# A gate ahead of a query product, and a mixture's step behind a projection, in an attention and mixture-of-experts block

## The chip, the cores and the metric

The kernel runs on one core of a Trainium2 chip. The metric is device microseconds of one execution, as the median of several runs. Before the change three runs gave 1143.45 us as their median (1142.99 to 1148.04). Engines are named as in the profile: PE is TensorE (PEld its weight loads), DVE is VectorE, ACT is ScalarE, POOL is GpSimd, SP is SyncE, whose queue issues most DMAs.

## The reference

The input x has 8 sequences of 512 tokens and 512 channels, in float32. All of the work below is done in float32, but for the lists of the sort.

```
xn = layernorm(x)
q, k, v = rotate(silu(xn @ Wq)), rotate(silu(xn @ Wk)), xn @ Wv     # 16 heads of 32
o  = decayed linear attention in chunks of 128 tokens:
     scores = (q @ k.T) * D ; state S = lam * S + (k * decay).T @ v
     o = scores @ v + (q * decay) @ S
gate = xn @ Wg1 @ Wg2
s  = rmsnorm_per_head(o * sigmoid(gate)) * weight @ Wo
f  = sum over the 4 best of 16 experts of weight * swiglu(xn) + shared expert * sigmoid(..)
out = x + s * silu(f)
```

## The kernel before, in words

The kernel has four stages. First, all tokens are normed, routed and sent through the shared expert, beside sequence 0's attention. Second, sequence 1's attention runs, and beside it `table` builds the lists that sort tokens into blocks of one expert: VectorE compares (L526, L529, L533), ScalarE numbers (L542), PE multiplies (L565, a bank "a" or "d" for each of eight rounds) and VectorE adds the result up (L576 for the first round, L574 later). Third, the experts' blocks run. Fourth, sequences 2 to 7 run their attention, and beside it GpSimd gathers the experts' results for each tile of 128 tokens.

The attention of a sequence b goes through four groups g of four heads. `key` and `query` (both through `rotated`) make a product of four steps on PE (pk, pq, L659), a Silu on ScalarE (L669) and four VectorE instructions (L671 to L675). `by_token` transposes keys (L691) into the one kept bank "k", which also holds the states' products (L714); the states' scan is L729. `scores` fills four banks "a" (ps, L725), which VectorE empties with the decay mask (sc, L750). `output` makes po (L761 or L766, then L772) in a bank "d", and VectorE multiplies it with the gate in L776. `value` makes pv (L615). `gate_2` makes the four tiles of the gate (L645, named p in the profile) in four banks and ScalarE puts a Sigmoid of each into `on` (L649).

PSUM has eight banks under four tags: four "a", one "k", one "m" (key products, first expert products, even value tiles), two "d" (query products, outputs, projections, odd value tiles, rounds 3 and 5 of the lists). A new tile takes a free bank of its tag or waits until the old tile's readers are done.

The order on PE is written out by hand: everything under `on_pe()` is chained behind what was emitted before it. On the other engines, what is emitted under `behind(engine)` follows the last instruction emitted for that engine; the rest is placed by a list scheduler. Between the steps of a product in sequence 1, `between[0]()` advances `table` by one piece.

In stage four the attention of a sequence calls `step` (here `advance`) at places of its own. Each call moves every active tile's `mixture` on by one piece: four gathers (L1325), one in each of four calls, a GpSimd add (L1331), a second add (L1334) with a VectorE combination (L1336), a VectorE add (L1340), a Silu (L1343), and for the tiles of sequences 0 and 1 the end `last`, with VectorE's L1363. New tiles are started at five in eleven calls. The projection of sequence b-1 is put off into sequence b: `project_tiles(before, ...)` makes pw (L817) of one tile in a bank "d" and `finish` calls `last`, whose L1363 multiplies the mixture's result by pw and so frees the bank. The output's add (L1367, GpSimd) is put on a list `late` with the number of steps so far, and is issued by the second call of `advance` after that.

For each group the order in `sequence` is: `scores`, a step, the next key (or value), `by_token`, one deferred projection (groups 0 and 1), a step, the next query (or value), [the gate, in group 0, where it has not been made], a second deferred projection, `output`, a step. Only sequences 0 and 1 make the gate here; sequence 2's is made at the beginning of the blocks, and from sequence 3 on the gate is made at the end of the sequence before.

Of the kernel before, what the change touches and what calls it, by code (L numbers as in the profile page):

```python
# [38 lines left out]
FIRST = 2  # L39
# [58 lines left out]
def tile_block(ctx: ExitStack, tc: tile.TileContext, a: dict, out: bass.AP):  # L98
# [8 lines left out]
    def bank(tag, name):  # L107
        return pp.tile([P, 512], F32, tag=tag, name=name, bufs={"a": 4, "k": 1, "m": 1, "d": 2}[tag])
# [101 lines left out]
    @contextmanager  # L210
    def on_pe():

        with tc.issue_after(last_pe[-1]) if last_pe else nullcontext():
            yield
        traced = nc.cur_bb.bb.instructions
        last_pe.append(next(
            i for i in reversed(traced) if i.engine == mybir.EngineType.PE))
# [374 lines left out]
    def home(b):  # L592
        return other[0] if other and (b - FIRST) % 2 else att

    def load_xT(b, pool=None):
        xT = (pool or home(b)).tile([P, KC, N], F32, tag="xT", name=f"xT_{b}", bufs=1)
        nc.sync.dma_start(xT.rearrange("p k n -> p (k n)"), xT_d[b])
        xT_of[b] = xT
# [4 lines left out]
    v_of, on_of, kT_of, qT_of, qd_of, sc_of, st_of, g1_of, rs_of, kd_of = ({} for _ in range(10))  # L603
# [5 lines left out]
    def value(b, t):  # L609
        if t == 0:  # L610
            v_of[b] = att.tile([P, NC, D], F32, tag="v", name=f"v_{b}", bufs=2)
        pv = bank("d" if t % 2 else "m", f"pv_{b}_{t}")
        for k in range(KC):
            with on_pe():
                nc.tensor.matmul(  # L615
                    pv, lhsT=xT_of[b][:, k, t * P : (t + 1) * P], rhs=wv[:, k, :],
                    start=(k == 0), stop=(k == KC - 1))
            between[0]()
        nc.scalar.copy(v_of[b][:, t, :], pv)
# [16 lines left out]
    def gate_2(b, tiles=range(NC), banks="aaaa"):  # L636
        if 0 in tiles:
            on_of[b] = home(b).tile([P, G, N], F32, tag="on", name=f"on_{b}", bufs=1)
        g1 = g1_of[b]
        p2s = {t: bank(banks[t], f"p2_{b}_{t}") for t in tiles}  # L640
        with on_pe():
            for g in range(G):
                for t in tiles:
                    tq = slice(t * Q, (t + 1) * Q)
                    nc.tensor.matmul(  # L645
                        p2s[t][:, g * P : (g + 1) * P], lhsT=wg2[tq, g * P : (g + 1) * P],
                        rhs=g1[tq, :], start=True, stop=True)
        for t in tiles:
            nc.scalar.activation(  # L649
                on_of[b][:, :, t * P : (t + 1) * P],  # L650
                p2s[t].rearrange("p (g n) -> p g n", n=P), AF.Sigmoid)
        if NC - 1 in tiles:
            g1_of.pop(b)
# [24 lines left out]
    def key(b, g, ps=None):  # L678
        kT_of[g] = rotated(b, g, "k", wk, ps)

    def query(b, g):
        qT_of[g] = rotated(b, g, "q", wq)

    def by_token(b, g):

        if not kept:
            kept.append(bank("k", f"pk_{b}_{g}"))
        pk = kept[0]
        with on_pe():
            for c in range(NC - 1):  # L690
                nc.tensor.transpose(  # L691
                    pk[:, c * P : (c + 1) * P], kT_of[g][:, c * C : (c + 1) * C], ident)
        kd = scr[0].tile([P, NC - 1, HG, HD], F32, tag="kd", name=f"kd_{b}_{g}")
        by_chunk = pk[:, : (NC - 1) * P].rearrange("p (c h d) -> p c h d", c=NC - 1, d=HD)
        for j in range(HG):
            nc.scalar.activation(
                kd[:, :, j, :], by_chunk[:, :, j, :], AF.Copy,
                scale=dk[:, g * HG + j : g * HG + j + 1])
        kd_of[g] = pk[:, (NC - 1) * P :], kd
# [55 lines left out]
    def output(b, g):  # L755
        po = bank("d", f"po_{b}_{g}")
        st, qd, sc = st_of.pop(g), qd_of.pop(g), sc_of.pop(g)
        with on_pe():
            for c in range(1, NC):
                if carry:  # L760
                    nc.tensor.matmul(  # L761
                        po[:, c * C : (c + 1) * C], lhsT=st[:, c - 1, :], rhs=qd[:, c - 1, :],
                        start=(c == 1), stop=False)
                for j in range(0 if carry else HG):
                    hs = slice(j * HD, (j + 1) * HD)
                    nc.tensor.matmul(  # L766
                        po[hs, c * C : (c + 1) * C], lhsT=st[hs, c - 1, :], rhs=qd[hs, c - 1, :],
                        start=(c == 1), stop=False)
            for c in range(NC):
                for j in range(HG):  # L770
                    h = g * HG + j
                    nc.tensor.matmul(  # L772
                        po[j * HD : (j + 1) * HD, c * C : (c + 1) * C],
                        lhsT=v_of[b][:, c, h * HD : (h + 1) * HD],
                        rhs=sc[j][:, c], start=False, stop=(c == NC - 1))
        nc.vector.tensor_tensor(on_of[b][:, g, :], po, on_of[b][:, g, :], ALU.mult)  # L776
# [16 lines left out]
    def inverse(b):  # L793
        nc.vector.reciprocal(rs_of[b], rs_of[b])
# [18 lines left out]
    def project(b, t):  # L813
        pw = bank("d", f"pw_{b}_{t}")
        with on_pe():
            for g in range(G):
                nc.tensor.matmul(  # L817
                    pw, lhsT=on_of[b][:, g, t * P : (t + 1) * P], rhs=wo[:, g, :],
                    start=(g == 0), stop=(g == G - 1))
        return pw  # L820
# [36 lines left out]
    def sequence(b, step, projected, before=None, defer=False, also=lambda: None):  # L857


        n = b + 1  # L860

        def project_tiles(q, ts):
            if q is not None:
                for t in ts:
                    projected(q, t, project(q, t))


        fill = ([0], [1], [2], [3], [], [], [], [])
        for g in range(G):
            scores(b, g)  # L870
            late_step = b == 0 and g + 2 >= G
            if not late_step:
                step()
            if g + 2 < G:
                key(b, g + 2)
            else:
                value(n, 2 * (g - 2))
            if late_step:
                step()
            if g + 1 < G:  # L880
                by_token(b, g + 1)
            project_tiles(before, fill[2 * g])
            step()
            if g + 2 < G:
                query(b, g + 2)
                if g + 3 == G and n not in xT_of:
                    load_xT(n)
            if g + 2 == G:
                value(n, 1)
            if g == 0 and b not in on_of:  # L890
                gate_2(b)
            project_tiles(before, fill[2 * g + 1])
            if fill[2 * g + 1] == [NC - 1]:
                on_of.pop(before, None)
            output(b, g)
            if defer and g + 2 == G:
                gate_1(n)
            step()
        v_of.pop(b)
        if n == FIRST:  # L900
            for _ in range(4):
                next(filling)
            gate_1(n)
            next(filling, None)
            for e in range(E - LATE // 2, E):
                nc.sync.dma_start(wexp[:, e, :], a["experts"][:, e, :])
            squares(b)
            inverse(b)
            value(n, 3)
            normed(b)  # L910
            experts_of_blocks()
            return
        if defer:
            gate_2(n)
        value(n, 3)
        also()
        squares(b)
        step()
        inverse(b)
        key(n, 0)  # L920
        also()
        query(n, 0)
        normed(b)
        also()
        if not defer:
            step()
        key(n, 1)
        by_token(n, 0)
        if defer:
            step()  # L930
        query(n, 1)
        also()
        if not defer:
            gate_1(n)
            project_tiles(b, [0, 1])
            also()
            project_tiles(b, [2, 3])
            also()
            on_of.pop(b)
        step()  # L940
# [156 lines left out]
    along()  # L1097
    enter(0, along)
    sequence(0, along, spill, also=lambda: next(sorting, None))
    for _ in sorting:  # L1100
        pass
# [14 lines left out]
    next(filling)  # L1116
    between[0] = lambda: next(filling, None)
    sequence(1, lambda: None, spill)
    between[0] = lambda: None
    slot = slots[0]  # L1120
# [354 lines left out]
```

## Time and profile before

| | |
|---|---|
| median of three runs | 1143.45 us (1142.99 to 1148.04) |
| the profiled execution | 1133.33 us |
| its span | 1131.5 us |
| PE busy | 1109.5 us (98%) |
| DVE busy | 753.3 us (67%) |
| ACT busy | 427.6 us (38%) |
| POOL busy | 446.2 us (39%) |
| sequence 1's first group to its last list product, about | 224 to 279 us |
| stage four's sequences 2 to 7, about | 689 to 1130 us |

A line of a timeline gives start and duration in us, engine, line, operation, output<-input and shape; in square brackets stands the idle time of the engine before it and who ended that. A line of the waits gives engine, its tile and line, whom it waited for, the total in us, how often, and the longest. A line of a window gives its bounds, its length, then for each of PE, PEld, DVE, ACT and POOL the busy time and in brackets the count; then the granted TensorE clock as a share of full speed, the share of the DMA engines, and GB/s. The timeline joins neighbouring instructions of one kind; a matmul's end is modelled, so times from one start to the next start are the safer measure.

### The profile page before, as it was taken

To read this page: it belongs to the slowest core of one execution; us is meant where nothing else is said; L and a number is where in the kernel's file an instruction comes from. 1 tells how busy PE (TensorE), PEld (TensorE's weight loads), DVE (VectorE), ACT (ScalarE), POOL (GpSimd) and SP (SyncE) were. 2 spreads that over 40 slices of the span, in tenths; PEclk is the share of its full clock that TensorE was granted. 3 is DMA by queue.
4 is the path that set the end of the run, shared out by engine and by line. 5 is a ranking of instruction groups with operands and counts; after the bars stand their busy time and mean duration, and the time that the engine had idled before them with its cause. 6 is when DMAs were issued, how large, how long until landed. Compare 5 with 4: busy or idle time off the path is not lost. (4 is left out here: it accounts for less than half of the span.)

```text
span 1131.5 us, 21658 instructions
## 1 busy us (share of the span) xinstructions
PE 1109.5 (98%) x7838; PEld 682.4 (60%) x7838; DVE 753.3 (67%) x1608; ACT 427.6 (38%) x924; POOL 446.2 (39%) x430
## 2 busy tenths in 40 slices
PE   7999999999999999999999999999999999999998
PEld 4445554455577777777777885655645545546453
DVE  6357744998354455555555666978789597797774
ACT  3223525255433333333333442352432523423541
POOL 4312100200333333333332314836868858768111
PEclk9999999999999999999999999999999999999999
DMA  9895341192779999999999986714648537444012
GB/s 343 311 334 187 138 161 48 57 378 88 215 208 237 236 234 238 234 239 239 241 238 267 245 203 244 270 57 160 232 121 258 156 114 250 138 138 143 11 38 75
DMA packets 163932, 218.50 MB, mean 193 GB/s; under 512 B 89840, under 2 KB 99184, under 8 KB 161776
## 3 DMA queue, kind: packets, MB, share of 16 engines
q1 hardware_dynamic: 142704, 146.76, 42.0%
q0 software_dynamic: 21120, 70.34, 24.2%
q8 instruction: 64, 1.05, 0.4%
q14 instruction: 44, 0.36, 0.1%
HBM read 126.78 MB, written 72.43 MB: 176 GB/s over the span
## 5 line engine op out<-in xcount | busy, mean ns | idle before, releaser
L1226 PE MATMUL pgu<-xts,wst 128*128 128x256 f32 x896 | 202.6, 379 | 0.0
L1226 PEld LDWEIGHTS pgu<-xts,wst 128*128 128x128 f32 x896 | 170.1, 190 | 46.2 <-issue 13.4
L1325 POOL DMA_INDIRECT yg<-y_d,place x128 | 141.6, 1106 | 30.3 <-issue 19.1
L1157 POOL DMA_INDIRECT more<-xn_d,slot x69 | 65.5, 949 | 220.1 <-DVE w L1210 107.5
L1241 PE MATMUL py<-wexp,slb 128*128 x272 | 129.9, 593 | 0.0
L1245 DVE TENSOR_SCALAR y<-py,w 128x512 f32<-128x512 f32 x136 | 102.0, 751 | 41.8 <-PE py L1241 35.4
L615 PE MATMUL pv<-wv,xT 128*128 128x512 f32 x256 | 118.3, 603 | 0.0
L659 PE MATMUL pk<-xT,wk 128*128 128x512 f32 x256 | 118.1, 603 | 0.0
L659 PE MATMUL pq<-xT,wq 128*128 128x512 f32 x256 | 115.7, 593 | 0.5 <-PEq L1289 0.5
L1232 ACT ACTIVATE slb<-pgu 128x256 f32<-128x256 f32 (+1 forms) x80 | 28.1, 351 | 219.8 <-PE pgu L1226 216.4
L817 PE MATMUL pw<-wo,on 128*128 128x512 f32 x224 | 102.3, 604 | 5.1 <-DVE m L1363 4.3
L1157 POOL DMA_INDIRECT xg<-xn_d,slot x67 | 63.6, 949 | 98.8 <-DVE w L1210 44.0
L1233 DVE TENSOR_TENSOR slb<-slb,pgu 128x256 f32<-128x256 f32 (+1 forms) x80 | 30.5, 381 | 105.3 <-ACT slb L1232 101.4
L1367 POOL TENSOR_TENSOR xo<-xo,m 128x512 f32<-128x512 f32 x31 | 45.6, 1470 | 134.2 <-DVE m L1363 126.7
L1208 DVE COPY wst<-wexp 128x512 f32 x160 | 61.7, 426 | 41.0 <-DVE y L1245 24.5
L1190 ACT COPY xts<-pl 128x512 uint16<-128x512 uint16 x110 | 84.3, 769 | 0.3 <-DMA pl<-xg 0.2
L659 PEld LDWEIGHTS pq<-xT,wq 128*128 128x128 f32 x256 | 47.2, 190 | 54.4 <-issue 53.0
L750 DVE TENSOR_TENSOR sc<-ps,dmask 128x512 f32<-128x512 f32 x128 | 79.0, 676 | 0.9 <-PE ps L725 0.9
L659 PEld LDWEIGHTS pk<-xT,wk 128*128 128x128 f32 x256 | 46.2, 189 | 50.7 <-issue 48.3
L615 PEld LDWEIGHTS pv<-wv,xT 128*128 128x128 f32 x256 | 45.9, 190 | 49.7 <-issue 46.7
L817 PEld LDWEIGHTS pw<-wo,on 128*128 128x128 f32 x224 | 41.8, 193 | 55.5 <-issue 46.2
L734 ACT COPY blocked<-state 32x96 f32<-32x96 f32 x96 | 30.8, 321 | 83.0 <-DVE state L729 82.2
(193 smaller groups left out, 1728.4 us busy)
## 6 DMA issues: line engine op xcount, KB each, us to landing
y_d<-y SPq DMA_DIRECT2D x136, 256.0 KB
wexp<-in_experts SPq DMA_DIRECT2D x16, 768.0 KB
sh_d<-sh SPq DMA_DIRECT2D x32, 256.0 KB
xT<-xT_d SPq DMA_DIRECT2D x8, 1024.0 KB
m<-sh_d SPq DMA_DIRECT2D x32, 256.0 KB
xo<-in_x SPq DMA_DIRECT2D x32, 256.0 KB
out<-xo SPq DMA_DIRECT2D x31, 256.0 KB
x<-in_x SPq DMA_DIRECT2D x7, 1024.0 KB
```

The lines of the kernel that those rows point to most:

```text
L615: nc.tensor.matmul(pv, lhsT=xT_of[b][:, k, t * P : (t + 1) * P], rhs=wv[:, k, :], start=(k == 0), stop=(k == KC - 1))
L659: nc.tensor.matmul(ps, lhsT=w[:, k, g * P : (g + 1) * P], rhs=xT_of[b][:, k, :], start=(k == 0), stop=(k == KC - 1))
L750: masked[:] = [nc.vector.tensor_tensor(s, pss[j].rearrange("p (c t) -> p c t", t=C), dmask[:, g * HG + j].unsqueeze(1).to_broadcast([P, NC ...
L817: nc.tensor.matmul(pw, lhsT=on_of[b][:, g, t * P : (t + 1) * P], rhs=wo[:, g, :], start=(g == 0), stop=(g == G - 1))
L1157: nc.gpsimd.indirect_dma_start(out=row(i), out_offset=None, in_=xn_d, in_offset=bass.IndirectOffsetOnAxis(ap=slot[:, i : i + 1], axis=0))
L1190: (nc.vector.tensor_copy if j in by_dve else nc.scalar.copy)(xt[:, u, KP:, :].bitcast(U16).rearrange("p k (t h) -> p h k t", h=2), pls[j % ...
L1208: nc.vector.tensor_copy(to, wflat[:, bass.ds(off + u * KC * F, KC * F)])
L1226: nc.tensor.matmul(pg[:, o * n * P : (o + 1) * n * P], lhsT=wst[j % 2][k // KP][:, (k % KP * 2 + o) * F :][:, :F], rhs=xt[:, :, k, :], sta ...
L1241: nc.tensor.matmul(py, lhsT=hT[:, u * P : (u + 1) * P], rhs=wflat[:, bass.ds(off + KC * 2 * F, D)], start=True, stop=True)
L1245: gone.append(nc.vector.tensor_scalar(y, py, w[:, u : u + 1], None, ALU.mult).ins)
L1325: nc.gpsimd.indirect_dma_start(out=yg, out_offset=None, in_=y_d, in_offset=bass.IndirectOffsetOnAxis(ap=place[:, r, g : g + 1], axis=0))
L1367: nc.gpsimd.tensor_tensor(xo, xo, m, ALU.add)
```

## The change

Two places of `sequence` are edited.

In sequences 3 to 6 (`b > FIRST`, FIRST is 2), in group 0, the step that stood right behind `scores` is taken from there and made behind the first deferred projection and its `last`, directly ahead of the step that already stood there. The number of steps is the same, and so are the tiles' pieces in each step, but for the output's add of the first projection, which goes by the number of steps and so is issued one step earlier.

In sequence 1, the gate is made ahead of query (1,2) and not behind it, and its fourth tile takes the bank "m" of the key products in place of a fourth bank "a". The old call is still there and finds the gate made. In sequence 0, where `b` is zero, nothing is changed.

```diff
         for g in range(G):
             scores(b, g)
             late_step = b == 0 and g + 2 >= G
-            if not late_step:
+            behind_tile = b > FIRST and g == 0
+            if not late_step and not behind_tile:
                 step()
             if g + 2 < G:
                 key(b, g + 2)
...
             if g + 1 < G:
                 by_token(b, g + 1)
             project_tiles(before, fill[2 * g])
+            if behind_tile:
+                step()
             step()
+            if g == 0 and b and b not in on_of:
+                gate_2(b, banks="aaam")
             if g + 2 < G:
                 query(b, g + 2)
```

## The prediction

> **What bounds the kernel now.** I read the page's busy times and chain first, then TensorE's waits, then timelines and clock windows around the two places that the diff touches.
>
> ```profile
> PE 1109.5 (98%) x7838; PEld 682.4 (60%) x7838; DVE 753.3 (67%) x1608; ACT 427.6 (38%) x924; POOL 446.2 (39%) x430
> PE 27%; DVE 10%; issue 1%; ACT 1%; DVEq 0%
> PE pw L817 <- DVE m L1363: 4.3, 4, 1.9
> PE p L645 <- DVE wexp L576: 1.4, 1, 1.4
> ```
>
> PE is busy for nearly the whole span, so a reorder can win only what PE loses in waits, and what the clock loses behind them. TensorE's waits list two that concern the diff: the second sequence's gate (p, L645), once 1.4 us, and the deferred projection (pw, L817), four times, 4.3 us together.
>
> Place one, sequence 1, from PE's timeline, a clock window and VectorE's timeline:
>
> ```profile
> 234.26 0.71 PE L645 MATMUL p<-g,wg 32*128 32x128 f32 x8
> 236.33 1.15 PE L645 MATMUL p<-g,wg 32*128 32x128 f32 x24 [1.37 <-DVE wexp L576]
> 237.42 0.92 PE L766 MATMUL po<-qd,state 32*32 32x128 f32 x24
> 239.00:240.00 1.00, 1.00 (x28) 0.92 (x24) 1.00 (x3) 1.00 (x3) 0.00 (x0) 0.50 0.99 412
> 245.56 0.42 DVE L526 TENSOR_TENSOR wexp<-count,sp 128x512 f16<-128x512 f16 x1 [0.54 <-PE pn L565]
> 277.87 1.13 PE L565 MATMUL pn<-wexp 128*64 128x286 f16 x8 [0.80 <-DVE wexp L529]
> ```
>
> A quarter of the gate runs, then waits until L576 has copied the list product pn out of the bank that the gate's fourth tile needs. Start to start it takes 237.42-234.26 = 3.16 us; the gate of sequence 6 takes 1.10 (965.13 to 966.23). So 2.06 are lost, and then the granted clock is 0.5 (sixth number): the next po, state and score products take 4.61 us start to start (237.42 to 242.03), the same three later 3.09 (265.33 to 268.42), 1.52 more. But VectorE is busy for 24.00 and 24.96 us of the windows 225:250 and 250:275, and PE meets it again at 277.87.
>
> Place two, sequences 4 and 6: PE, then VectorE.
>
> ```profile
> 848.10 3.70 PE L817 MATMUL pw<-wo,on 128*128 128x512 f32 x8 [1.14 <-DVE m L1363]
> 865.75 3.70 PE L817 MATMUL pw<-wo,on 128*128 128x512 f32 x8 [0.15 <-DVE m L1363]
> 1001.48 5.40 PE L817 MATMUL pw<-wo,on 128*128 128x512 f32 x8 [1.91 <-DVE m L1363]
> 865.01 0.68 DVE L1363 TENSOR_TENSOR m<-m,pw 128x512 f32<-128x512 f32 x1
> 997.53 0.74 DVE L1336 SCALAR_TENSOR_TENSOR m<-m,sg,yg 128x512 f32<-128x512 f32 x1
> 1000.74 0.68 DVE L1363 TENSOR_TENSOR m<-m,pw 128x512 f32<-128x512 f32 x1
> ```
>
> The second projection waits for VectorE's L1363 to free the first one's bank. A pq or pw takes 3.44 us to the next start, so the true waits are 1.30 (sequence 4: 843.36+3.44 to 848.10), 1.29 (sequence 5: 919.20 to 923.93) and 2.07 (sequence 6: 995.97 to 1001.48); sequence 3 has none. Only the 2.07 is followed by half clock: that pw takes 5.23 to the next start against 3.53 in sequence 4, 1.70 more.
>
> **The change part by part.** No instruction is added or dropped; I take the order of each engine's queue from the code.
>
> *The gate.* It now follows the transposes that end at 229.4. Its three banks are score banks, freed by L750 one by one until 229.2; the fourth is the keys' bank, free when ScalarE's Silu (229.30, 0.60) ends at 229.9. Behind the gate on PE are queued query (1,2), its pn and po, so at most 0.5 us is new wait. The pn product then takes the fourth score bank and nobody waits for L576. PE gains up to 2.06+1.52 = 3.58. VectorE does not: from 221.6 to 277.8 it waits twice, 0.33 at 236.94 (for the Silu of that query) and 0.54 at 245.56 (for pn). The second goes, since pn comes earlier. The first stays, since the query now ends at 234.3+1.8 = 236.1, about where its Silu ran (236.30). So PE reaches 277.87 early and waits longer there. I take 0.54 gained. The best bound is 0.87 with both idles gone, or 3.58 if VectorE's order were not what ends it. The worst: the gate's Sigmoid now sits between two Silus, so a table load (row at 236.91, 1.28) may fall between pq and its Silu, which would cost VectorE 1.28-0.54 = 0.74, and the longer wait at 277 may bring half clock (1.52): 2.26 lost.
>
> The page "ScalarE: Activation LUTs", What ACT_TABLE_LOAD costs, speaks against this order: it puts a switch of tables at about 2.66 us, load and drain. The trace has the Sigmoid at 238.21, right behind the load; by the page the loss would be 1.38 larger, by the trace it is not.
>
> *The step.* In sequences 3 to 6 one step moves from before key (b,2) to behind the first projection's L1363. Its VectorE rows, start to start: sequence 3 L1340 (767.29) 0.61; sequence 4 L1363 and L1336 (843.09 to 844.36) 1.27; sequence 5 L1336 (918.94 to 920.66) 1.72; sequence 6 L1336 (997.53 to 998.20) 0.67. By that much L1363 comes earlier. Sequence 5's wait of 1.29 goes, sequence 4's 1.30 nearly, sequence 6's becomes 2.07-0.67 = 1.40.
>
> Where does it go? In sequence 4 VectorE's rows touch from 826.87 to 865.69, and the instructions before the third projection's L1363 (865.01) are the same in both orders; PE waits there until 865.75 either way. I take 0. Sequence 5 is the same: the state scan L729 (934.19), behind which the transposes wait (0.36), has the same work ahead of it. I take 0. In sequence 6 VectorE catches up (idle 0.51 at 1006.91), so 0.67 stays. Whether the clock still drops: waits of 1.29 and 1.30 kept it, 2.06 and 2.07 lost it; 1.40 is nearer to the first, so I take the 1.70 as gained. Together 2.37.
>
> The page "TensorE: Matmul & The Clock Gate", What's actually happening, says that the clock falls after an idle window of some 3.4 us; here it fell behind waits of about 2.06. By the page no wait of this size costs clock, and sequence 6 would give 0.67 alone.
>
> *What else moves with the step.* GpSimd's queue: the first projection's output add (L1367) is delayed by step count, so it is now issued one step earlier, ahead of three GpSimd instructions. In sequence 4 these ran at 834.15, 835.53 and 837.07 (1.36+1.27+1.13 = 3.76 us) while GpSimd would otherwise have idled until 843.86; now they wait for L1363 (846.8). Followed on by its rows, GpSimd is some 4 us late at 874. The first reader is VectorE's L1336 at 865.61, which needs the add of 857.87; that now ends near 864.6, so 1.0 us of cover is left. In sequences 5 and 6 the delay is about 1 us, in 3 about 1.5, before VectorE's idle stretches. SyncE's loads of the step (m, xo) run ahead (12 and 4 buffers). ScalarE's Silu of the step has only m behind it. A GpSimd add that meets a two-input VectorE operation stretches it (L675 2.04 at 835.32 against 0.69): adds that move may stretch other rows or none, 1.35 either way, in sequence 4 and in 5.
>
> **Sum.** 0.54 + 0 + 0 + 2.37 = 2.9 us. The profiled execution took 1133.33 (span 1131.5) and would take 1130.4; the median of three runs is 1143.45, 10.1 above it, and I carry the saving over: 1140.5. About 0.5% (5.7 us) is what a measurement of this kernel tells from no change, so this is "same".
>
> **The rivals.** *All waits close*: VectorE's order is not the bound, so PE keeps the gate's 3.58, sequence 4's 1.30 and the 0.31 at 865.75, sequence 5's 1.29 and the 0.53 before 934.59 (930.53+3.53), sequence 6's 2.07+1.70: 10.8 us, 1132.7. For it: the scheduler may reorder what is not pinned. Against: VectorE's touching rows. Chance 0.14.
>
> *Nothing is won but the shift*: 1.40 still drops the clock in sequence 6, and the gate's gain is lost to the Silu behind the table load: 0.67-0.74, 1143.5. Chance 0.10.
>
> *GpSimd becomes the bound (slower)*: at VectorE's L1336 in sequence 4, and at the same place in 5, it is later than the cover of 1.0 us by the rest of its 4 us: 3.0 each, on VectorE's bound stretch, and PE's wait then passes 2.06 and brings half clock, 1.70 each: 9.4 lost, less the 2.9, 1150.0. It decides if the add behind L1336 ends after 865.6. For it: GpSimd is busy 21 of 25 us there. Against: the rows leave the 1.0, and sequence 5's delay is small. Chance 0.10.
>
> **How the numbers follow.** The forecast (part of the waits closes) has 0.66. Its own bounds: best 0.87 + 2.37 + twice 1.35 = 5.9, 1137.5; worst -2.26 + 0.67 - twice 1.35 = -4.3, 1147.7. Two rivals lie outside with 0.24 together, more than 2 in 10, so the range reaches part of the way to the faster one: 1135.5 to 1148.0. Faster by over 0.5% is the first rival, 0.14; slower is the third, 0.10; the rest 0.76.
>
> **What would show it.** Right: the L645 wait on L576 is gone and the clock stays at 1.0 at 238 to 242; PE's wait for VectorE at the list products near 277 is over 0.8; the second projection of sequences 4 and 5 has no wait, yet their third or fourth has about what was saved; sequence 6's L817 takes about 3.7 instead of 5.40 behind a wait near 1.2 by the profile's count. Wrong: new idle time on VectorE's L1336 or L1340 for GpSimd's adds (third rival), a half clock elsewhere, or sequences 4 and 5 shorter by over 1 us each (first rival).

## The result: 0.56% slower

The changed kernel took 1151.1 us (median of 12 runs, 1147.2 to 1153.85) where the kernel before took 1143.22 (12 runs): ratio 1.0056, 95% interval 1.0039 to 1.0073. The forecast was 1140.5, 2.9 us faster, with a range of 1135.5 to 1148.0, and "same" for what stays within some 0.5%. The loss is clear of zero and a little over that 0.5%, the sign is the other one, and the time lies outside the range. Each group of runs below has its own runs of the kernel before, and that took 1132 to 1145 us from group to group. So ratios and traces are compared within a group, or by the lengths of single sequences.

The page of the changed kernel answers to the page shown before: its busy times.

```profile
PE 1120.5 (97%) x7838; PEld 687.1 (60%) x7838; DVE 753.3 (65%) x1608; ACT 428.2 (37%) x924; POOL 444.9 (39%) x430
```

VectorE's instructions are the same, and in these two traces its busy time too; that is chance, for in the two traces without issue gaps below it is 748.4 before and 761.7 changed. TensorE is busy for 11 us more, with the same instructions: slower rows, not more of them. TensorE's waits in the same trace (tile and line, whom it waited for, total, times, longest):

```profile
PE pk L714 <- issue: 5.2, 11, 1.2
PE pk L691 <- DVE state L729: 2.9, 1, 2.9
PE pw L817 <- DVE m L1368: 2.2, 1, 2.2
```

The four waits for the deferred projection's bank (4.3 us) have become one of 2.2. The gate's wait is gone. New are 2.9 us at L691, the transposes of the blocked keys, which wait for VectorE's state scan L729, and 5.2 us at L714 put down to issue, which means that the profile shows nothing that PE waited for. Behind line 888 the changed kernel's line numbers are five higher: the first projection's product is L1368, the mixture's multiply-add L1341, its second sum L1345, GpSimd's pair adds L1336 and L1339, its output add L1372.

Place one, sequence 1: PE's timeline and a clock window, then ScalarE's and VectorE's timelines.

```profile
230.66 1.63 PE L645 MATMUL p<-g,wg 32*128 32x128 f32 x32
239.00:240.00 1.00, 1.00 (x56) 0.96 (x51) 1.00 (x2) 1.00 (x5) 0.00 (x0) 1.00 1.05 436
244.05 1.23 PE L565 MATMUL pn<-wexp 128*64 128x286 f16 x16 [0.92 <-DVE sc L750]
278.32 1.12 PE L565 MATMUL pn<-wexp 128*64 128x286 f16 x8 [0.88 <-DVE wexp L529]
237.34 1.28 ACT L669 ACT_TABLE_LOAD   x1 [1.96 <-PE pq L659]
235.74 0.42 DVE L526 TENSOR_TENSOR wexp<-count,sp 128x512 f16<-128x512 f16 x1 [0.23 <-PE pn L565]
```

All 32 gate products run as one row, 1.56 us to the next start (230.66 to 232.22) against 1.10 for the gate of sequence 6, so the new waits stay under the 0.5 that was forecast, and the clock stays at 1.0. A later list product now waits 0.92 for a score bank, and at 278 PE meets VectorE again (0.88). The table load does fall between pq and its Silu, but VectorE does not wait there: its only wait around the query, 0.23, is for the list product behind the moved gate.

The rest is read from the lengths of the sequences: from the first product of one sequence's squares (L786) to the next one's, read off PE's timeline of each trace, in us.

| trace | sequence 3 | 4 | 5 | 6 |
|---|---|---|---|---|
| before, first trace | 73.99 | 75.85 | 75.96 | 79.68 |
| before, again | 73.98 | 75.90 | 75.99 | 76.99 |
| changed, first trace | 76.00 | 84.73 | 82.24 | 75.34 |
| changed, again | 73.99 | 80.05 | 82.07 | 76.29 |
| gate alone | 73.99 | 75.86 | 76.16 | 79.70 |
| step alone | 73.99 | 78.46 | 80.85 | 76.34 |
| all, output add kept late | 73.98 | 77.20 | 74.82 | 76.31 |
| gate, step in 6 alone | 73.99 | 75.89 | 75.98 | 76.29 |
| output add early, nothing else | 76.26 | 79.34 | 80.77 | 77.09 |
| step in 5 and 6, add late | 74.58 | 79.36 | 77.07 | 75.54 |

Sequences 4 and 5 lose and 6 gains. Sequence 3 takes 73.98 or 73.99 in every trace that has no issue gaps; three of these traces have them in stage four, the changed kernel's first (6.5 us) and the last two (5.9 and 4.2). The first traces differ by more than the medians do (spans 1150.5 and 1131.5, medians 7.9 apart): the profiled execution of before took 1133.33, less than any of its timed runs there, and the changed kernel's holds 6.5 us of gaps put down to issue in stage four, 0.2 to 1.2 us each, which its second trace has not.

### The profile page after: what moved, and what is told of

Read it like the earlier page. It is cut to its first block, busy times and chain, and to the rows that moved or that the text cites. A ratio compares the mean times of both kernels' runs of the same rounds, so it can differ in the third digit from the quotient of the medians.

```text
span 1150.5 us, 21659 instructions
## 1 busy us (share of the span) xinstructions
PE 1120.5 (97%) x7838; PEld 687.1 (60%) x7838; DVE 753.3 (65%) x1608; ACT 428.2 (37%) x924; POOL 444.9 (39%) x430
## 5 line engine op out<-in xcount | busy, mean ns | idle before, releaser
L615 PE MATMUL pv<-wv,xT 128*128 128x512 f32 x256 | 121.4, 616 | 0.0
L1372 POOL TENSOR_TENSOR xo<-xo,m 128x512 f32<-128x512 f32 x31 | 44.2, 1427 | 153.0 <-DVE m L1368 144.9
L750 DVE TENSOR_TENSOR sc<-ps,dmask 128x512 f32<-128x512 f32 x128 | 79.3, 678 | 3.0 <-PE ps L725 2.2
```

Of the source, the lines that this page charges most:

```text
L615: nc.tensor.matmul(pv, lhsT=xT_of[b][:, k, t * P : (t + 1) * P], rhs=wv[:, k, :], start=(k == 0), stop=(k == KC - 1))
L750: masked[:] = [nc.vector.tensor_tensor(s, pss[j].rearrange("p (c t) -> p c t", t=C), dmask[:, g * HG + j].unsqueeze(1).to_broadcast([P, NC ...
L1372: nc.gpsimd.tensor_tensor(xo, xo, m, ALU.add)
```

## The experiments

Three theories. Theory 1: the moved step lets the first projection's output add into GpSimd's queue one step earlier; it waits at the head for VectorE, and what stands behind it then runs beside VectorE's busiest rows and lengthens them. Theory 2: VectorE's own order is worse. Theory 3: the gaps put down to issue.

### The halves apart

Gate alone:

```
-            behind_tile = b > FIRST and g == 0
+            behind_tile = False
```

> Only the second sequence's gate is moved; the mixtures' step stays where it was. Theory 1 (GpSimd's order: the moved step lets the first projection's output add into GpSimd's queue one step earlier, the adds and gathers behind it fall on VectorE's busiest stretch and lengthen its rows): the loss is all in sequences four and five, so this kernel is 0.5 to 1.5 us faster than before, with the squares of sequences two to five 74, 76, 76 us apart as before. Theory 2 (VectorE's own order: the moved rows come too late for the projections): the same, 0.5 to 1.5 us faster. Theory 3 (TensorE's gaps put down to issue, 0.24 to 1.2 us each, which the changed kernel's profile has and the one before has not, come from the gate's move or from the build): 3 to 8 us slower, and those gaps appear in sequences two to five here too.

Measured: 1131.49 against 1132.13, ratio 0.9991 (0.9967 to 1.0015). Sequences 3 to 6 are as before, with no gaps. The gate is worth nothing that can be measured.

Step alone:

```
-            if g == 0 and b and b not in on_of:
-                gate_2(b, banks="aaam")
```

> Only the mixtures' step is moved, in sequences three to six; the gate stays. Theory 1 (GpSimd's order) and theory 2 (VectorE's order): 8 to 9 us slower than before, squares four to five about 84.5 us apart where they were 76, five to six about 82 where they were 76, six to seven about 75 where they were 80 (the numbers of the sequences' ends by the profile). Theory 3 (gaps from the gate's move): 2 to 4 us faster than before, with no gaps put down to issue.

Measured: 1139.95 against 1132.13, ratio 1.0061 (1.0037 to 1.0085), without a gap put down to issue in its trace. Sequences 4 and 5 take 78.46 and 80.85, less than the 84.5 and 82 expected, which were read from the trace with the gaps. The whole loss is in the step's move, and theory 3 isn't needed for it.

### The output add put back

```
-            late.append((steps[0], add))
+            late.append((steps[0] + (FIRST < b + 1 < B - 1 and t == 0), add))
```

> The whole change, with one difference: the output add of the first projection's tile waits one step longer, so that it stands in GpSimd's queue where it stood before the change. VectorE's order stays that of the change. Theory 1 (GpSimd's order): the loss of sequences four and five is gone, 1137 to 1141 us, and GpSimd's adds start again before VectorE's stretch between the scores and the third projection. Theory 2 (VectorE's order): 1149 to 1152 us as the changed kernel, with VectorE's rows in sequence four as long as there. Theory 3: as the changed kernel, since the gate is moved here too.

Measured: 1133.13 against 1132.13, ratio 0.9996 (0.9975 to 1.0016). One step of delay for one add in each of four sequences takes the 0.6% away, with VectorE's order as changed. Theory 1 holds for most of it: sequence 5 goes from 80.85 to 74.82. In sequence 4 half of the loss stays (77.20 against 75.85). There the product with the first projection and the older mixture's product now follow each other on VectorE (0.59 apart, where they were 4.27 apart), so GpSimd's two output adds come as a pair beside VectorE's sums. That part goes with VectorE's order as changed, as theory 2 has it. This is read from the trace; no run puts that order back by itself.

### The same by itself

The kernel before, with nothing moved but that add:

```
-            late.append((steps[0], add))
+            late.append((steps[0] - (FIRST < b + 1 < B - 1 and t == 0), add))
```

> The kernel before, with the gate and the step where they were; only the output add of the first projection's tile is let into GpSimd's queue one step earlier, as the change does by the way. By the build's order this alters GpSimd's queue in sequences three, five and six; in sequence four the order stays, since an older add stands ahead. Theory 1 (GpSimd's order is the cause): sequence five grows by 3 to 5 us (75.96 to 79 to 81 between the squares), with a wait of 2 to 4 us for VectorE's scan at the blocked keys' transposes; the others within 0.5 us; whole 3 to 5 us slower. Theory 2 (VectorE's order, by the moved halves of the mixtures): as before, within 1 us.

Measured: 1149.36 against 1142.65, ratio 1.0047 (1.0023 to 1.0072). GpSimd's timeline, then PE's, in sequence 5:

```profile
932.49 1.65 POOL L1367 TENSOR_TENSOR xo<-xo,m 128x512 f32<-128x512 f32 x1 [5.13 <-DVE m L1363]
935.54 1.27 POOL L1331 TENSOR_TENSOR yg<-yg,yg 128x512 f32<-128x512 f32 x1
946.85 0.55 PE L691 MATMUL pk<-ident,kT 128*128 128x128 f32 x3 [3.54 <-DVE state L729]
```

The output add waits 5.13 us at the head of the queue, the pair add runs behind it, and PE waits 3.54 us at L691 where the first trace of before had 0.36. Sequence 5 takes 80.77, as theory 1 forecast. So by the medians the add's place costs about what the change costs, with VectorE's order as it was. Not forecast was that 3 and 4 grow too, by 2.3 and 3.4. In 4 that isn't the add: the order there is that of before, and in the same group of runs the kernel that leaves sequence 4 alone (step in 5 and 6) takes 79.36 for it; both have 1.3 us of issue gaps there. How much of sequence 3's 2.3 is the add's, beside 1.1 of gaps, stays open.

### The same pair without issue gaps

> The kernel before, for its trace beside that of the changed kernel on one chip. Theory 1: sequences three to six at 74, 76, 76 and 78 to 80 us between the squares, as in the first trace, with VectorE the releaser of every wait of TensorE's over 0.3 us. If TensorE's gaps put down to issue belong to a chip and not to a kernel, they are there in this kernel too wherever it takes 1143 us, 4 to 6 us in all, and absent where it takes 1132.

> The changed kernel once more. Theory 1: 0.4% to 0.8% slower than before on any chip; in its trace GpSimd's adds reach into VectorE's stretch between the scores and the blocked keys in sequences four and five, with waits of 1.7 to 4 us at the blocked keys' transposes and of 2.2 at the third or fourth projection. Theory 3 (gaps by issue cost the time): slower only where the gaps stand in its trace and not in that of before on the same chip.

Measured: before 1129.72 (one run), changed 1139.12 against 1132.79, ratio 1.0049 (1.0031 to 1.0067). Neither trace has a gap put down to issue in stage four, and the loss is there. This pair shows the mechanism best. Sequence 5 before (first trace): GpSimd, then VectorE.

```profile
918.90 1.27 POOL L1331 TENSOR_TENSOR yg<-yg,yg 128x512 f32<-128x512 f32 x1
923.95 1.64 POOL L1367 TENSOR_TENSOR xo<-xo,m 128x512 f32<-128x512 f32 x1 [3.78 <-DVE m L1363]
932.21 1.51 POOL L1367 TENSOR_TENSOR xo<-xo,m 128x512 f32<-128x512 f32 x1 [1.24 <-DVE m L1363]
932.05 0.55 DVE L744 TENSOR_TENSOR qd<-qT,dq 128x384 f32<-128x384 f32 x1
933.12 1.15 DVE L1336 SCALAR_TENSOR_TENSOR m<-m,sg,yg 128x512 f32<-128x512 f32 x1
934.19 0.34 DVE L729 TENSOR_TENSOR_SCAN state<-carry,pk 128x96 f32<-128x96 f32 x1
```

The same in the changed kernel's second trace, with PE's two rows behind:

```profile
928.12 1.71 POOL L1372 TENSOR_TENSOR xo<-xo,m 128x512 f32<-128x512 f32 x1 [4.48 <-DVE m L1368]
931.23 1.28 POOL L1336 TENSOR_TENSOR yg<-yg,yg 128x512 f32<-128x512 f32 x1
936.62 2.48 POOL L1372 TENSOR_TENSOR xo<-xo,m 128x512 f32<-128x512 f32 x2
936.28 3.25 DVE L744 TENSOR_TENSOR qd<-qT,dq 128x384 f32<-128x384 f32 x1
940.05 2.17 DVE L1341 SCALAR_TENSOR_TENSOR m<-m,sg,yg 128x512 f32<-128x512 f32 x1
942.14 0.34 DVE L729 TENSOR_TENSOR_SCAN state<-carry,pk 128x96 f32<-128x96 f32 x1
942.54 0.90 PE L691 MATMUL pk<-ident,kT 128*128 128x128 f32 x3 [4.15 <-DVE state L729]
943.23 6.07 PE L817 MATMUL pw<-wo,on 128*128 128x512 f32 x8
940.00:950.00 10.00, 7.46 (x14) 3.48 (x14) 8.63 (x15) 3.52 (x10) 5.12 (x5) 0.66 0.62 204
```

Before, the pair add (918.90) runs first, and then GpSimd waits 3.78 for the output add. Changed, the output add stands ahead, so the pair add runs at 931.23, and all behind it follows without a pause: two output adds run as one stretch of 2.48 beside L744, which grows from 0.55 to 3.25, and the next pair add comes ahead of the scan too, where L1341 takes 2.17 instead of 1.15. PE then waits 4.15 at L691. The table adds up such growth: what VectorE's rows with both operands in SBUF, the engines' working memory (two-operand SBUF rows from here on), take beyond their undisturbed time (L673 0.67, L674 0.68, L675 0.69, L744 0.55, multiply-add 0.74, the other sums 0.68), from 21 us behind the squares to the scan L729, and when the scan starts behind the squares.

| trace | sequence 4: growth | scan at | sequence 5: growth | scan at |
|---|---|---|---|---|
| before, first trace | 2.68 | 37.63 | 5.36 | 40.29 |
| step alone | 6.00 | 40.22 | 7.44 | 42.39 |
| changed, again | 5.97 | 40.16 | 7.44 | 43.61 |
| all, output add kept late | 3.79 | 38.96 | 4.21 | 39.15 |

With the step alone sequence 5's rows grow by 2.08 more, and the scan is 2.10 later; with the add kept late they grow by 1.15 less, and scan and sequence are 1.14 earlier. The step alone makes the sequence 4.89 longer: 2.10 of VectorE, and 2.79 left for the half clock behind a wait of 3.85 at L691 (from 939.31, where that wait ends, to 944.99 the granted clock is 0.50, and half of 5.68 is 2.84). In the changed kernel's second trace VectorE comes into the stretch 1.24 later besides, the wait is 4.15, the clock falls to 0.66 over the window shown, and the sequence is 6.11 longer: 3.32 and 2.79.

In sequence 4 the waits at L691 and at the fourth projection are, in PE's timeline of the same trace:

```profile
859.03 0.55 PE L691 MATMUL pk<-ident,kT 128*128 128x128 f32 x3 [1.62 <-DVE state L729]
868.71 3.70 PE L817 MATMUL pw<-wo,on 128*128 128x512 f32 x5 [2.26 <-DVE m L1368]
```

The step alone shows it without half clock: the scan runs 2.59 later than before, the fourth projection starts 2.59 later (50.29 behind the squares against 47.70), and the sequence is 2.61 longer. The 1.14 that PE saved at the second projection it waits again, and what VectorE lost is the loss.

With the output add late, sequence 5 reads, GpSimd, VectorE, PE:

```profile
926.71 1.28 POOL L1336 TENSOR_TENSOR yg<-yg,yg 128x512 f32<-128x512 f32 x1
930.55 1.71 POOL L1372 TENSOR_TENSOR xo<-xo,m 128x512 f32<-128x512 f32 x1 [2.56 <-DVE m L1368]
938.72 0.55 DVE L744 TENSOR_TENSOR qd<-qT,dq 128x384 f32<-128x384 f32 x1
939.79 1.15 DVE L1341 SCALAR_TENSOR_TENSOR m<-m,sg,yg 128x512 f32<-128x512 f32 x1
941.26 0.55 PE L691 MATMUL pk<-ident,kT 128*128 128x128 f32 x3 [0.43 <-DVE state L729]
```

The pair add is ahead again, both rows are back at 0.55 and 1.15, and the wait is 0.43.

### Is it the add beside the row?

The kernel before, and the one with the step moved, each with GpSimd's three adds per tile on one column:

```
-            nc.gpsimd.tensor_tensor(ys[0], ys[0], ys[1], ALU.add)
+            nc.gpsimd.tensor_tensor(ys[0][:, :1], ys[0][:, :1], ys[1][:, :1], ALU.add)
...
```

> The kernel before with each of GpSimd's adds of the mixtures (two per tile, and the output add) on one column of 512 instead of all: the sums of the experts' outputs and of the residual are left out but for that column, and the queue's order and its waits stay. If VectorE's rows are long only because an add runs beside them, the rows of 1.1 to 2.1 us in sequences four to six go to 0.7, and the span falls by what waits on VectorE there now: 1 to 4 us. If they are long for their own reasons, nothing falls.

> The mixtures' step moved as in the change, the gate left, and each of GpSimd's adds of the mixtures on one column of 512 (the same sums left out as in the run beside it). Theory 1 with the adds' time as the price: the step now costs nothing, and this kernel is 2 to 4 us faster than the one with the small adds and the step unmoved, since the waits at the second projections go. If the price lies in the queue's waits and not in the adds beside VectorE's rows, or in VectorE's own order (theory 2): still 3 to 7 us slower than that one.

Measured: 1202.46 and 1205.15 against 1142.65, ratios 1.0538 (1.0507 to 1.0568) and 1.0546 (1.0519 to 1.0573). As a price for the step these two say nothing. They agree within their intervals, and something else fills them. VectorE's last rotary sum over a whole trace (minimum, median, maximum ns), first the kernel before, then the one with small adds, then the line with that one's longest gaps of PE:

```profile
L675 DVE TENSOR_TENSOR qT<-qT,swq x32: 670/692/2071, 77.9 to 1090.0; 128x512 f32<-128x512 f32 x32
...
L675 DVE TENSOR_TENSOR qT<-qT,swq x32: 672/691/693, 77.3 to 1158.6; 128x512 f32<-128x512 f32 x32
...
L629 PE MATMUL pg<-xT,wg 128*32 128x128 f32 x256 | 17.3, 304 | 10.0 <-issue 9.7
```

The maximum falls from 2071 to 693 ns, so the long rows are the adds' doing. But PE now has 24.4 us of gaps put down to issue in stage four, at a mean clock of 0.973 over the run. Gathers were running on GpSimd in 62% of that gap time, and in 27% of the time between the squares of sequences 2 and 7. Why PE pauses there stays open.

A second try was to keep GpSimd's pace: the changed kernel with each add made a copy of its second operand.

```
-            nc.gpsimd.tensor_tensor(xo, xo, m, ALU.add)
+            nc.gpsimd.tensor_copy(xo, m)
...
```

> The changed kernel with each of GpSimd's adds of the mixtures (two per tile and the output add) made a copy of its second operand: the sums are left out, the queue's order, its waits and about the time per instruction stay. Theory 1, if a one-operand instruction beside VectorE holds it less: VectorE's rows in sequences four and five go back towards 0.7 us, the waits at the blocked keys' transposes (1.6 and 4.1) and at the third projection (2.3) go, and both sequences take 74.5 to 75.5 us between the squares. If a copy holds VectorE as an add does, or if the waits in the queue are the cause and not the adds' time: 80 and 82 us as in the changed kernel. If, with the gathers coming sooner, TensorE's gaps put down to issue rise as with the adds on one column, the sequences are over 85 us.

Measured: 1172.61 against 1144.78, ratio 1.0256 (1.0213 to 1.0299); the sequences take 81.5, 90.6, 84.5 and 78.8. The copies take 0.68 to 0.83 us on average, not an add's 1.28, so the pace was not kept, and the gaps are 17.2 us. VectorE's rows are short beside the copies (L744 at most 0.71, against 3.25 in the changed kernel's second trace), and the waits for VectorE at L691 are gone, but the gaps cover the price here too. The last of the three outcomes named came, though of sequences 4 and 5 only 4 is over 85.

### Versions meant to be faster

The whole change with the step in sequence 6 alone:

```
-            behind_tile = b > FIRST and g == 0
+            behind_tile = b == 6 and g == 0
```

> The gate is moved and the mixtures' step is moved in sequence six alone. Theories 1 and 2: sequences three to five as before, sequence six about 4 us shorter as in the changed kernel, and the gate's 0.7 us: 1138 to 1139.5 us, faster than both kernels. Theory 3 (gaps from the gate's move or the build): 1143 to 1148 us, with the gaps in the sequences whose code is that of before.

Measured: 1130.03 against 1132.13, ratio 0.9979 (0.9957 to 1.0000). The gate unmoved, and the step in sequences 5 and 6 with the add kept late:

```
-            behind_tile = b > FIRST and g == 0
+            behind_tile = b in (5, 6) and g == 0
...
-            late.append((steps[0], add))
+            late.append((steps[0] + (b in (4, 5) and t == 0), add))
```

> The mixtures' step moved in sequences five and six alone, the first projection's output add kept at its old step there, the gate left where it was. Theory 1: sequence five 74.8 (1.1 less), six 76.3 (3.4 less), three and four as before: 1127.5 us on a chip where before takes 1132, ratio 0.996. Theory 2: sequence five 2 to 5 us longer, six 3.4 shorter: 1131 to 1134 us.

Measured: 1140.68 against 1142.65, ratio 0.9990 (0.9973 to 1.0007). Less than theory 1 forecast (0.996): its trace has no wait of PE at L691, but sequences 4 and 5 take 79.36 and 77.07 with 4.2 us of issue gaps in stage four, and so it neither confirms nor refutes the forecast of 74.8 for sequence 5. And every output add one step later, on top of the gate and the step in sequence 6:

```
-            late.append((steps[0], add))
+            late.append((steps[0] + 1, add))
```

> A version meant to be faster: the gate moved, the step moved in sequence six alone, and every output add of the mixtures' tiles, not only that of the first projection, let into GpSimd's queue one step later than before the change. Theory 1: GpSimd waits less at its head for VectorE's products, so the pair adds behind come before VectorE's full stretch: 2 to 5 us faster than before (with the move in sequence six alone it was 2.4). Against it: the later output adds may themselves fall beside VectorE's two-operand rows, then 0 to 3 us slower than the version with that move alone.

Measured: 1131.19 against 1132.79, ratio 0.9987 (0.9976 to 0.9998). Sequences 4, 5 and 6 take 76.17, 77.19 and 76.94, longer than with the step in 6 alone, and the later adds meet VectorE's rows as well (L744 takes 2.92 in sequence 4, L673 3.36 in 5). The gate with the step in sequence 6 alone is the best of these, 0.2% ahead of the kernel before, with an interval that ends at none.

## Why the prediction was wrong, step by step

**The gate**: read rightly on PE, not on VectorE. The wait is gone, the clock holds, PE waits 0.88 near 277 (forecast: over 0.8), and the table load falls where the lower bound feared. But the 0.54 that was to be won, VectorE's wait for the list product near 245, was no loss of its own: it stands in the three executions that lost their clock (0.54, 0.84 and 0.87), and in none of the four with the gate unmoved that kept it. With the gate moved, VectorE waits 0.23 to 0.25 for that product. In the seven traces with the gate moved, the stretch from sequence 0's squares to sequence 1's takes 86.81 to 86.83 us; unmoved it takes 87.55 to 87.61 where the clock fell and 86.54 to 86.56 where it did not. So the move gains some 0.75 where the clock would have fallen and loses 0.26 where not; 0.54 was taken.

**The half clock**: the sum took it as following from the wait's length (2.06 and 2.07 bring it, 1.30 doesn't). It does not. Seven executions have the gate's wait of 1.36 to 1.37 by the profile's count; three of them lose clock behind it (among them both traces of before) and four keep it. PE's wait, then clock windows of the step alone and of before again:

```profile
236.59 1.15 PE L645 MATMUL p<-g,wg 32*128 32x128 f32 x24 [1.37 <-DVE wexp L576]
...
235.00:240.00 5.00, 3.63 (x118) 3.08 (x119) 5.00 (x10) 4.30 (x9) 0.00 (x0) 1.00 1.02 423
...
235.00:240.00 5.00, 4.39 (x92) 3.68 (x95) 5.00 (x11) 4.12 (x9) 0.00 (x0) 0.66 1.01 422
```

The same holds in sequence 6, where before again runs its second projection at full clock behind a wait of 1.90:

```profile
1000.53 3.70 PE L817 MATMUL pw<-wo,on 128*128 128x512 f32 x8 [1.90 <-DVE m L1363]
```

That sequence takes 76.99 there, not 79.68. So the step in sequence 6 is worth 0.7 us in an execution that keeps its clock (76.99 to 76.3), which is the 0.67 of VectorE's row. The 1.70 for the clock (2.7 in fact, 79.68 less 76.99) is won only sometimes. A longer wait can keep the clock too. The early add alone has the 3.54 at L691 (946.85), and its clock window reads:

```profile
940.00:950.00 10.00, 6.46 (x18) 2.86 (x17) 10.00 (x13) 3.09 (x10) 9.26 (x8) 1.00 0.72 222
```

"TensorE: Matmul & The Clock Gate", What's actually happening, of the Trainium skill says that the activity window runs free of the kernel. The traces agree: in the changed kernel's first, for one, the half clock begins at 875.45, 899.34, 953.95 and 981.26 us, which are 7, 16 and 8 times 3.413 apart, and lasts 3.41 each time. That one such window without work is needed the runs refute, since 1.36 was enough. What decides between two waits of the same length, they do not show.

**The step in sequences 4 and 5**: this is the step that failed. "I take 0" was right about what PE saves: the 1.30 and 1.29 come back as waits for VectorE behind. But the collisions were taken as 1.35 either way with 0 as their value, and they came out one-sided and larger: VectorE 2.6 us later at the scan in sequence 4 and 2.1 to 3.3 in sequence 5, with 2.8 of half clock on top behind the waits of 3.85 and 4.15. Where the sum has 0 and 0, the step alone lost 2.61 and 4.89. The prediction saw the cause, the output add issued a step earlier, and followed it to the wrong neighbour. It asked whether VectorE's L1336 would wait for a late add (cover 1.0 us). On these stretches of sequences 4 and 5 VectorE never waited for GpSimd: the adds, once held back, came without pauses beside VectorE's two-operand rows, on the stretch where VectorE sets the pace. And for sequence 5 it called the delay "about 1 us": the pair add went from 25.0 to 32.7 us behind the squares.

"SBUF — State Buffer", Who interferes with whom, of the Trainium skill has the rule that bears on this: a VectorE instruction with two SBUF inputs and a GpSimd instruction that reads SBUF shut each other out for a whole instruction; one with a single SBUF input, outside the two-port modes, does not contend. The rows agree: L744 went from 0.55 to 3.25 beside adds of 2.48, and L776, which reads PSUM, took 0.68 with an add beside it and without. In all of stage four, in the trace of before and in the changed kernel's second, L776, L750 and the multiplication with pw, each with one operand in PSUM, never take over 0.69 us, while each kind of two-operand SBUF row has some of 1.3 us or more, up to 3.2. Read with that rule, an add's price hangs on which VectorE rows it meets, and it can be listed row by row; "either way" was no estimate.

**The rivals**: the third had the sign, the place (sequences 4 and 5) and about the time (1150.0), with a chance of 0.10. That the time fits is luck: its mechanism, VectorE waiting for GpSimd's add on its bound stretch, was not seen. "All waits close" was not seen either. Of the signs named as wrong, "a half clock elsewhere" came. "New idle time on VectorE" for GpSimd's adds came in a place where it costs nothing: late in sequence 3 the changed kernel's second trace has waits of 0.98, 2.61 and 1.56 where before has one of 0.91, and the sequence keeps its 73.99.

## What to carry to other kernels

When a step is moved, list what it lets through by count (here an add delayed by steps) and follow each such instruction to the engine that it runs beside, not only to its reader: an add that waits at the head of GpSimd's queue takes everything behind it from a stretch with room to one without. Before calling a stretch of VectorE "the same work", sum the two-operand SBUF rows in it and the GpSimd adds that will run beside them. A half clock seen in one trace behind one wait is not a price: look at a second trace.

## What was not expected of the hardware

- Who waits is not told by the recorded starts. In the trace of before an output add was recorded 0.16 us into L744 (932.21 and 932.05), and L744 kept its 0.55; in the changed kernel's second trace two were recorded 0.34 us into it (936.62 and 936.28), and it took 3.25, past the end of both. "SBUF — State Buffer", Who interferes with whom, of the Trainium skill says that the order of issue decides who blocks; the profile's starts on GpSimd are rough, so these two rows neither show nor refute it.
- The kernel before took 1132 us in two groups of runs and 1143 to 1145 in three, and one and the same chip gave 1132.79 in one group and 1144.78 in a later one. Where it took 1143, the traces of the kernels beside it have 4 to 6.5 us of gaps put down to issue before small matmuls in stage four; where it took 1132 they have none. The kernel before itself was traced only in executions of 1133.33 and 1129.72, which have none. With GpSimd's adds shortened, so that its gathers follow each other faster, such gaps reach 17.2 to 27.2 us. What PE lacks there was not found.
